# Six moves of x and the first queries' copy, put elsewhere in the order of a cross-attention kernel

## The chip, the cores and the metric

The kernel runs on one core of one Trainium2 chip. The metric is the device time of one execution in microseconds, as a median of several runs. Five engines work side by side, each through its own list in order: TensorE (PE, the matmuls), VectorE (DVE), ScalarE (ACT), GpSimd (POOL) and SyncE (SP). SP's list holds nearly all the DMA issues, so the order of the transfers is the order of SP's list. The work of each engine is written out by hand; nothing reorders it, and semaphores make an instruction wait until what it needs is there.

## What is computed

Layer norm of x, queries, attention over a memory of 256 slots whose keys and values are the same tensor, an output projection, and the residual. Batch 8, 256 queries, 256 slots, width 1024, 32 heads of 32, float32 throughout.

```python
mu = jnp.mean(hidden_states, axis=-1, keepdims=True)
var = jnp.var(hidden_states, axis=-1, keepdims=True)
x = (hidden_states - mu) * jax.lax.rsqrt(var + LN_EPS) * ln_gamma + ln_beta
Q = _split_heads(x @ Wq.T)
K = _split_heads(memory_keys)
V = _split_heads(memory_values)
scores = jnp.einsum('bhsd,bhtd->bhst', Q, K) * scale
mask = attention_mask[:, None, None, :]
scores = jnp.where(mask, scores, -jnp.inf)
probs = jax.nn.softmax(scores, axis=-1)
attn = jnp.einsum('bhst,bhtd->bhsd', probs, V)
...
out = attn @ Wout.T
return residual + out
```

## The kernel before

**Groups.** The work is cut into 64 groups: group n is batch n // 8 and four of its heads, that is 128 of the 1024 columns. For a group, PE makes the queries (L340), the scores of the four heads (L479, 128 queries by 256 slots, twice) and, two groups later, the values products (L622); DVE adds the mask and takes the minimum (L515), ACT takes the exponential and its sum (L519), DVE the reciprocal (L526), POOL multiplies by it (L528), and DVE transposes the probabilities in blocks of 32 (L534). The main loop's pass n holds, on PE, the scores of group n + 1, values of group n - 2, steps of the output projection (L694) and queries still to be made.

**Moves of probabilities.** The values products need half of the blocks in other partitions. ACT copies a part of them aside (`aside`, L540); then two DMAs move blocks within the tile pT (the first pair, L600) and two more bring in the copy (the second pair, L604). The second pair writes where the first has read, so it waits for the first to land. Between the two pairs SP issues what stands in the list `between`: the loads of later keys, values, x, output weights and residuals. All this is `tail`; for the first seven groups it is held back into the next group's softmax, from group 8 on it follows at once.

**x of a batch.** From the third batch on, x is normalized on ACT, transposed in blocks of 32 by DVE (`blocks_x`, L311, tile xe), and sixteen DMAs of 64 KB each (`move_x`, L327) bring the blocks to their partitions in tile xnT. The table `moves` says in which pass: for the third batch four in pass 5, six in pass 6, six in pass 7. They are issued behind the softmax of that pass. The first product that reads the third batch's xnT is the query of group 16, in pass 10.

**The start.** Before the loop, batch 0's x comes in halves of 128 queries. `transpose_x0` and `copy_x0` (L275 on ACT, L277 on DVE) bring it to tile xnT by eight chunks of 128 columns, `first_q` makes group 0's queries (L285) with a copy to qa by ACT (L289), and `scores(0, (0,))` the scores of the first half. The softmax of group 0 is a generator, so that the caller can put PE's and ACT's other work between its parts; `next(first)` runs it to its next `yield`. It carries a list `fill` of three pieces: statistics of batch 1's two halves (`ln_stats`: DVE L226, L229, L231, then a power on POOL, L234) and the normalization of its first half on DVE (`ln_norm`, L252). `fill_in()` takes the next piece. The second half is normalized by POOL (also L252) after the softmax of group 0, and PE transposes both halves (L302) at the end of pass 0.

SP's transfers share eight semaphores in turn.

Of the kernel before, what the change touches and what calls it, by code (L numbers as in the profile page):

```python
# [59 lines left out]
def xattn_kernel(  # L60
# [11 lines left out]
    nc = tc.nc  # L72
# [3 lines left out]
    NC = D // P  # L76
    NQ = NC
    NH = P // HD
# [191 lines left out]
    def copy_x0(s, c, engine):  # L270

        to, pt = xnT0[:, c, ts(s, P)], px0[s, c // (NC // 2)][:, c % (NC // 2), :]
        g, b = gam[:, c : c + 1], bet[:, c : c + 1]
        if engine is nc.scalar:
            nc.scalar.activation(to, pt, AF.Identity, bias=b, scale=g)  # L275
        else:
            nc.vector.tensor_scalar(to, pt, g, b, ALU.mult, ALU.add)  # L277

    def first_q(s, chunks=range(NC)):

        if s == 0:
            pqs[0] = ps_q.tile([P, 512], F32, tag="pq", name="pq_0")
        cols = ds(0, P) if s == 0 else ds(P, P + 1)
        for c in chunks:
            nc.tensor.matmul(  # L285
                pqs[0][:, cols], wq[:, 0, c, :], xnT0[:, c, cols],
                start=(c == chunks[0]), stop=(c == chunks[-1]),
            )
        nc.scalar.activation(qa[:, 0, cols], pqs[0][:, cols], AF.Copy, scale=NEG_SCALE)  # L289
# [194 lines left out]
    def softmax(*args):  # L484
        for _ in softmax_parts(*args):
            pass
# [4 lines left out]
    def softmax_parts(n, copies=(), ahead=(), between=(), hooks={}, fill=()):  # L491

        fill = list(fill)

        def fill_in():
            if fill:  # L500
                fill.pop(0)()

        pss = scs[n]
        pT = pTs[n] = ptp.tile([P, 2, NI, NH, NS, K], F32, tag="pT", name=f"pT_{n}")
        pc = asp.tile([P, NI, NH, NS, K], F32, tag="pc", name=f"pc_{n}")
        es, mns, dens = {}, {}, {}

        def exps(j, part=range(NS)):
            if 0 in part:
                es[j] = ep.tile([P, NS, T], F32, tag="e", name=f"e_{n}_{j}")  # L510
                mns[j] = sm.tile([P, NS], F32, tag="mn", name=f"mn_{n}_{j}")
                dens[j] = sm.tile([P, NS], F32, tag="den", name=f"den_{n}_{j}")
            e, mn, den = es[j], mns[j], dens[j]
            for s in part:
                nc.vector.tensor_tensor_reduce(  # L515
                    out=e[:, s, :], in0=pss[j][:, s, :], in1=mbs[n // NQ], scale=1.0,
                    scalar=NO_SCORE, op0=ALU.add, op1=ALU.min, accum_out=mn[:, s : s + 1],
                )
                nc.scalar.activation(  # L519
                    e[:, s, :], e[:, s, :], AF.Exp, bias=mn[:, s : s + 1], scale=-1.0,  # L520
                    accum_out=den[:, s : s + 1],
                )

        def normalize(j):
            rden = sm.tile([P, NS], F32, tag="rden", name=f"rden_{n}_{j}")
            nc.vector.reciprocal(rden, dens[j])  # L526
            for s in range(NS):
                nc.gpsimd.tensor_scalar(  # L528
                    es[j][:, s, :], es[j][:, s, :], rden[:, s : s + 1], 1.0,
                    ALU.mult, ALU.mult,  # L530
                )

        def blocks(j):
            nc.vector.transpose(  # L534
                pT[:, :, :, j, :, :].rearrange("p a i s k -> p (a i) s k"),
                es[j].rearrange("p s (b t) -> p b s t", t=K),
            )

        def aside(j):
            nc.scalar.copy(pc[:, :, ts(j, 2)], pT[:, 1, :, ts(j, 2)])  # L540

        if n == 0:
            for j in range(NH - 1):
                exps(j, (0,))
            yield
            exps(NH - 1, (0,))
            fill_in()
            yield
            for j in range(NH):
                exps(j, (1,))  # L550
            normalize(0)
            fill_in()
        else:
            exps(0)
            while tails:
                tails.pop()()
            late = "p1" in hooks
            if not late:
                for done in list(pvs):
                    copy_at(done)  # L560
            exps(1)
            for hook in hooks.get("soon", ()):
                hook()
            exps(2)
            normalize(0)
            for hook in hooks.get("p1", ()):
                hook()
            exps(3)
            if late:
                for done in list(pvs):  # L570
                    copy_at(done)
        copies = list(copies)
        for copy in copies[: NQ if n <= NQ else 1 if n == NQ + 1 else 0]:
            copies.remove(copy)
            copy()
        for hook in hooks.get(0, ()):
            hook()
        normalize(1)
        fill_in()
        blocks(0)  # L580
        for hook in hooks.get(1, ()):
            hook()
        normalize(2)
        fill_in()
        blocks(1)
        aside(0)
        normalize(3)
        fill_in()
        blocks(2)
        while fill:  # L590
            fill_in()
        for copy in copies:
            copy()

        def tail():
            blocks(3)
            aside(1)

            for r in range(2):
                nc.sync.dma_start(pT[ts(2 * r, K), 1], pT[ts(2 * r + 1, K), 0])  # L600
            for load in between:
                load()
            for r in range(2):
                nc.sync.dma_start(pT[ts(2 * r + 1, K), 0], pc[ts(2 * r, K)])  # L604

        for load in ahead:
            load()
        if n < NQ or N - NQ < n < N - 1:
            tails.append(tail)
        else:  # L610
            tail()
        yield
# [16 lines left out]
    def copy_at(n):  # L629
        b, c = divmod(n, NQ)  # L630
        k, c = divmod(c, NK)
        if c == 0:
            ats[b, k] = atp.tile([P, NK, NS, NA, K], F32, tag="at", name=f"at_{b}_{k}")
        for r, pv in enumerate(pvs.pop(n)):
            nc.scalar.copy(  # L635
                ats[b, k][:, c, :, ts(r, 2), :], pv.rearrange("p a s k -> p s a k")
            )
# [136 lines left out]
    for n in range(N):  # L774
# [12 lines left out]
    loads, stats, norms, trans, moves, biases, masks = (  # L787
        {n: [] for n in range(N)} for _ in range(7)
    )
    for b in range(1, B):  # L790
        first = NQ * (b - 1) + 2
        if b == 1:
            when = dict(moves=())
        elif b == 2:
            when = dict(
                loads=(0, 1), stats=(2, 3), norms=(3, 3), trans=(4, 5),
                moves=tuple(5 + (i + 2) // 6 for i in range(16)),
            )
        else:
# [4 lines left out]
                moves=tuple(first - 6 + (i + 2) // 6 for i in range(16)),  # L804
# [60 lines left out]
    transpose_x0(1)  # L865
    scores(0, (0,))
    for c in range(NC):
        copy_x0(1, c, nc.scalar if c < NC // 2 else nc.vector)
    first = softmax_parts(0, (partial(copy_q, 1), partial(copy_q, 2)), (), (), {}, [
        partial(ln_stats, 1, 0), partial(ln_stats, 1, 1),  # L870
        partial(ln_norm, 1, 0, nc.vector),
    ])
    next(first)
    first_q(1)
    make_q(1, second=True, chunks=range(2))
    next(first)
# [9 lines left out]
    for b in range(B - 1):  # L886
        done, ends = 0, b == B - 2
        for i, counts in enumerate(ENDS if ends else STEPS):
            n = NQ * (b + 1) + i
# [15 lines left out]
    for n in range(N):  # L905
        b, i = divmod(n - NQ, NQ)
        new_q = new_qs[n]
        between = []
# [5 lines left out]
        if n + 3 in firsts or n + 2 in firsts:  # L914
            between, ahead = between + ahead, []
# [11 lines left out]
            between.append(partial(load_wo, which, pair))  # L927
        if n == NQ - 1:
            between.append(partial(load_res, 0, 0, 0))
        if n == N - 4:  # L930
            again = xp.tile([P, NS, D], F32, tag="x", name="x_again")
            for s in range(NS):
                between.append(partial(nc.sync.dma_start, again[:, s, :], x[B - 1, ts(s, P), :]))
# [88 lines left out]
        if N - NQ + 2 < n < N - 1:  # L1022

            c = n - (N - NQ + 3)
# [104 lines left out]
```

## Time and profile before

| | us |
|---|---|
| median of 3 runs | 577.44 (575.85 to 577.75) |
| profiled execution, device time | 575.24 |
| its span | 573.5 |
| PE busy | 565.9 (99%) |
| DVE busy | 459.2 (80%) |
| ACT busy | 412.3 (72%) |
| POOL busy | 403.8 (70%) |
| DMA queue of SP, share of 16 engines' span | 68.9% |

A line of the time line gives the start and the duration in microseconds, the engine, the line of the kernel, the operation, the tiles written and read, the shape, and how many instructions were merged; in brackets stands how long the engine had been idle before and what ended that. SPq are issues of transfers: the transfer itself lands later. PE's matmuls overlap, so the sum of durations in a row can exceed the time to the next row. In the list of waits a line names who waited, for what, the total in microseconds, how often, and the longest.

### The profile page before, as it was taken

The numbers are of one execution on the slowest core, as the hardware profiler recorded it, in microseconds if no ns is written. First come the engines' busy times: TensorE is split into PE (matmuls) and PEld (weight loads), VectorE is DVE, ScalarE is ACT, GpSimd is POOL, SyncE is SP. The second block draws the span as 40 slices with busy tenths as digits, with TensorE's granted clock in tenths as the row PEclk, the third lists the DMA queues.
The fourth block names the chain that finished last, engine by engine and source line by source line (L and its number), as shares of the span: only waits on it lengthen the run. The fifth ranks groups of instructions, "written<-read, shape, count | busy, mean of one in ns | idle before, by whom it ended". The sixth has DMA issues, their size and how long they took to land.

```text
span 573.5 us, 20000 instructions
## 1 busy us (share of the span) xinstructions
PE 565.9 (99%) x7162; PEld 392.1 (68%) x7162; DVE 459.2 (80%) x1698; ACT 412.3 (72%) x1424; POOL 403.8 (70%) x675
## 2 busy tenths in 40 slices
PE   8999999899999999999999999999999999999997
PEld 8788876566667677677676677667766777755444
DVE  6897987788877879888888888888877868879823
ACT  4688886767758867698667967769767876869920
POOL 1788898789896896776567675666657667448780
PEclk9999999999999999999999999999999999999999
DMA  8675877766678667877787767886768774536751
GB/s 299 238 201 189 241 216 216 240 186 189 192 239 273 195 181 220 248 241 204 202 239 208 214 196 192 251 263 190 181 177 258 210 228 141 142 101 180 212 162 74
DMA packets 47475, 117.98 MB, mean 206 GB/s; under 512 B 9104, under 2 KB 9872, under 8 KB 47376
## 3 DMA queue, kind: packets, MB, share of 16 engines
q1 hardware_dynamic: 47088, 116.69, 68.9%
q8 instruction: 57, 0.93, 0.7%
q14 instruction: 42, 0.34, 0.2%
q10 hardware_dynamic: 288, 0.01, 0.0%
HBM read 65.28 MB, written 11.53 MB: 134 GB/s over the span
## 4 chain that ended last, share of the span: by engine, by line
PE 86%; POOL 4%; DVE 4%; DMA 2%; ACT 1%; issue 1%; SPq 1%; DVEq 0%; ACTq 0%; POOLq 0%
PE po_S L694 20%; PE pq_A L440 16%; PE pv L622 11%; PE sc L479 10%; PE po_A L694 10%; PE pq L340 7%; PE pq_S L440 6%; PE po_end L761 3%; POOL e L528 3%; DVE e L515 2%; DMA pT<-pT 1%; PE po_last L761 1%; ACT e L519 1%; PE busy L120 1%; DVE pT L534 1%
## 5 line engine op out<-in xcount | busy, mean ns | idle before, releaser
L528 POOL TENSOR_SCALAR e<-e,rden 128x256 f32<-128x256 f32 x512 | 235.8, 478 | 128.7 <-DVE rden L526 127.0
L519 ACT ACTIVATE e<-e,mn 128x256 f32<-128x256 f32 x512 | 254.1, 501 | 51.2 <-DVE mn L515 50.8
L534 DVE STREAM_TRANSPOSE pT<-e 128x512 f32<-128x512 f32 x256 | 180.7, 707 | 53.1 <-POOL e L528 35.5
L515 DVE CUSTOM_DVE_ANT_0 e<-sc,mb 128x256 f32<-128x256 f32 x512 | 185.9, 416 | 26.9 <-PE sc L479 26.4
L540 ACT COPY pc<-pT 128x512 f32<-128x512 f32 x128 | 79.0, 617 | 68.7 <-DVE pT L534 41.2
L519 ACT ACTIVATION_READ_ACCUMULATOR e<-e,mn 128x1 f32 x512 | 97.9, 191 | 0.0
L340 PE MATMUL pq<-xnT,wq 128*128 128x256 f32 (+1 forms) x368 | 84.2, 383 | 2.1 <-DMA xnT<-xe 2.1
L340 PEld LDWEIGHTS pq<-xnT,wq 128*128 128x128 f32 x368 | 68.6, 190 | 16.8 <-issue 6.9
L622 PE MATMUL pv<-pT,v 64*32 64x128 f32 x4096 | 74.8, 274 | 1.0 <-issue 0.8
L622 PEld LDWEIGHTS pv<-pT,v 64*32 64x32 f32 x4096 | 57.1, 105 | 26.7 <-issue 12.7
L479 PEld LDWEIGHTS sc<-k,qa 32*128 32x128 f32 x1024 | 46.2, 184 | 42.4 <-issue 23.2
L694 PE MATMUL po_S<-wo,at 128*128 128x512 f32 x152 | 74.3, 606 | 0.0
L479 PE MATMUL sc<-k,qa 32*128 32x256 f32 x1024 | 73.6, 400 | 0.1
L694 PE MATMUL po_A<-wo,at 128*128 128x512 f32 x128 | 60.9, 609 | 0.0
L694 PE MATMUL po_S<-wo,s 128*128 128x512 f32 x104 | 50.1, 606 | 0.0
L526 DVE RECIPROCAL rden<-den 128x2 f32<-128x2 f32 x256 | 37.6, 147 | 6.0 <-ACT e L519 4.8
L515 DVE DVE_READ_ACCUMULATOR2_ANT mn<- 128x1 f32 x512 | 42.4, 83 | 0.0
L440 PEld LDWEIGHTS pq_A<-xnT,wq 128*128 128x128 f32 x320 | 37.3, 192 | 4.8 <-issue 4.1
L694 PEld LDWEIGHTS po_A<-wo,at 128*128 128x128 f32 x128 | 22.5, 189 | 24.6 <-issue 22.7
L694 PEld LDWEIGHTS po_S<-wo,at 128*128 128x128 f32 x152 | 25.8, 190 | 19.8 <-issue 19.1
L440 PE MATMUL pq_A<-xnT,wq 128*128 128x128 f32 x320 | 37.3, 275 | 0.0
L635 ACT COPY at<-pv 128x128 f32<-128x128 f32 x128 | 26.2, 254 | 8.2 <-PE pv L622 8.2
(95 smaller groups left out, 605.1 us busy)
## 6 DMA issues: line engine op xcount, KB each, us to landing
v<-in_kv_dram SPq DMA_DIRECT2D x32, 512.0 KB, 4.4
pT<-pT SPq DMA_DIRECT2D x128, 128.0 KB, 2.9
pT<-pc SPq DMA_DIRECT2D x128, 128.0 KB, 4.1
ring<-kept_T SPq DMA_DIRECT2D x18, 512.0 KB, 5.3
k<-in_kv_dram SPq DMA_DIRECT2D x32, 256.0 KB, 3.7
x<-in_x_dram SPq DMA_DIRECT2D x14, 512.0 KB, 5.6
r<-in_x_dram SPq DMA_DIRECT2D x28, 256.0 KB, 5.1
out_dram<-r SPq DMA_DIRECT2D x28, 256.0 KB, 2.5
```

What stands on the lines that cost most here:

```text
L340: nc.tensor.matmul(pqs[n], wq[:, o, c, :], xnTs[b](c), start=(c == 0), stop=(c == NC - 1),)
L440: nc.tensor.matmul(pqs[b][:, o, :], w[:, c], x_[:, c], start=begins and o + c == 0, stop=c == NK - 1, skip_group_check=True,)
L479: nc.tensor.matmul(scs[n][j][:, s, :], qa[r, n % NQ, ts(s, P)], ks[n - n % 2][r, n % 2, :], start=True, stop=True,)
L515: nc.vector.tensor_tensor_reduce(out=e[:, s, :], in0=pss[j][:, s, :], in1=mbs[n // NQ], scale=1.0, scalar=NO_SCORE, op0=ALU.add, op1=ALU.m ...
L519: nc.scalar.activation(e[:, s, :], e[:, s, :], AF.Exp, bias=mn[:, s : s + 1], scale=-1.0, accum_out=den[:, s : s + 1],)
L526: nc.vector.reciprocal(rden, dens[j])
L528: nc.gpsimd.tensor_scalar(es[j][:, s, :], es[j][:, s, :], rden[:, s : s + 1], 1.0, ALU.mult, ALU.mult,)
L534: nc.vector.transpose(pT[:, :, :, j, :, :].rearrange("p a i s k -> p (a i) s k"), es[j].rearrange("p s (b t) -> p b s t", t=K),)
L540: nc.scalar.copy(pc[:, :, ts(j, 2)], pT[:, 1, :, ts(j, 2)])
L622: nc.tensor.matmul(pvs[n][r][j * HD : (j + 1) * HD], vs[n - n % 2][ts(r, 2 * K), i, ds(n % 2 * P + j * HD, HD)], pT[ts(r, 2 * K), :, i, j, ...
L635: nc.scalar.copy(ats[b, k][:, c, :, ts(r, 2), :], pv.rearrange("p a s k -> p s a k"))
L694: nc.tensor.matmul(po, operand(b, name)[:, c], wo[:, which, c], start=begins and c == 0, stop=c == NK - 1, skip_group_check=not begins,)
```

## The change

Three edits. In the softmax of group 0 the exponentials of all four heads of the first half are issued in one stretch, with one `yield` behind them, and the `fill_in()` that stood behind the fourth is gone. The caller's first `next(first)` goes too, so `first_q(1)`, with its copy on ACT, and two chunks of the next queries come ahead of all these exponentials. The three pieces of `fill` are then taken behind `normalize(0)`, `normalize(1)` and `normalize(2)`; before, they were taken behind the fourth exponential of the first half, `normalize(0)` and `normalize(1)`.

The eight copies of the second half of batch 0's x go to ACT and DVE in turn; before, ACT had the first four and DVE the last four.

In pass 7 (NQ is 8) the six moves of the third batch's x are put at the head of `between`, ahead of the load of values and of a residual, and so between the two pairs of moves of group 8's probabilities; the table's entry is emptied, so they are not issued again behind the softmax.

```diff
         if n == 0:
-            for j in range(NH - 1):
+            for j in range(NH):
                 exps(j, (0,))
-            yield
-            exps(NH - 1, (0,))
-            fill_in()
             yield
             for j in range(NH):
                 exps(j, (1,))
...
     for c in range(NC):
-        copy_x0(1, c, nc.scalar if c < NC // 2 else nc.vector)
+        copy_x0(1, c, nc.vector if c % 2 else nc.scalar)
     first = softmax_parts(0, (partial(copy_q, 1), partial(copy_q, 2)), (), (), {}, [
         partial(ln_stats, 1, 0), partial(ln_stats, 1, 1),
         partial(ln_norm, 1, 0, nc.vector),
     ])
-    next(first)
     first_q(1)
     make_q(1, second=True, chunks=range(2))
     next(first)
...
         if n == NQ - 1:
             between.append(partial(load_res, 0, 0, 0))
+            between[:0] = [partial(move_x, *args) for args in moves[n]]
+            moves[n] = []
```

## The prediction

> **What bounds the kernel now.** First the page's head, for how much room TensorE (PE) has; then the list of waits, for where the rest goes; then the time lines round each place that the change touches.
>
> ```profile
> span 573.5 us, 20000 instructions
> PE 565.9 (99%) x7162; PEld 392.1 (68%) x7162; DVE 459.2 (80%) x1698; ACT 412.3 (72%) x1424; POOL 403.8 (70%) x675
> ...
> PE pq L340 <- DMA xnT<-xe: 2.1, 1, 2.1
> ```
>
> PE is idle for 573.5 - 565.9 = 7.6 us in all. One wait of 2.1 us is for the moves of x (the columns are the total, how often, the longest). It is the third batch's first query product; PE's time line has it:
>
> ```profile
> 99.32 1.22 PE L622 MATMUL pv<-pT,v 64*32 64x128 f32 x64
> ...
> 103.70 3.69 PE L340 MATMUL pq<-xnT,wq 128*128 128x256 f32 x16 [2.11 <-DMA xnT<-xe]
> ```
>
> At 99.32 stand the values products of group 8, which need both pairs of moves of group 8's probabilities. Without the wait, the query product would start 103.70 - 2.11 - 99.32 = 2.27 us after them. SyncE's queue (SP) before this, and what it waited for:
>
> ```profile
> 85.55 0.43 SPq L173 DMA_DIRECT2D wo<-in_woT_dram  x1
> ...
> 87.33 1.19 SPq L600 DMA_DIRECT2D pT<-pT  x2
> 88.57 0.57 SPq L144 DMA_DIRECT2D v<-in_kv_dram  x1
> 89.19 0.49 SPq L150 DMA_DIRECT2D r<-in_x_dram  x1
> 94.61 1.95 SPq L604 DMA_DIRECT2D pT<-pc  x2
> 96.61 3.75 SPq L327 DMA_DIRECT2D xnT<-xe  x6
> ...
> SPq L604 <- DMA pT<-pT: 4.8, 1, 4.8
> ...
> SPq L327 <- DMA wo<-in_woT_dram: 2.2, 1, 2.2
> ```
>
> Group 8's first pair is issued at 87.33, then v and r; the second pair (94.61) stands 4.8 us until the first has landed; only then come the six moves, 0.63 us apart. The last line shows a move of x that waits 2.2 us for a weight load with which it shares no data: eight semaphores go round among SP's transfers, so an issue also waits until the one eight issues before it has landed.
>
> At the start GpSimd (POOL) is the pace:
>
> ```profile
> 15.96 0.55 POOL L234 TENSOR_TENSOR rstd<-ve,mhalf 128x1 f32<-128x1 f32 x1 [6.72 <-DVE ve L231]
> ...
> 19.02 1.11 POOL L234 TENSOR_TENSOR rstd<-ve,mhalf 128x1 f32<-128x1 f32 x1 [0.67 <-DVE rden L526]
> 20.12 2.74 POOL L528 TENSOR_SCALAR e<-e,rden 128x256 f32<-128x256 f32 x6
> 22.85 3.78 POOL L252 TENSOR_SCALAR x<-x,mv,rstd 128x1024 f32<-128x1024 f32 x1
> ...
> 26.63 1.03 PE L302 MATMUL px<-ring,x 128*128 128x128 f32 x8
> ```
>
> POOL normalizes the second half of batch 1's x until 26.63, and PE's transposes of it start right there; from there the chain of what ended last runs through POOL's next normalizations, DVE and ACT to PE's first values product at 36.66.
>
> **The start, part by part.** *Copies in turn.* Now ACT does four from 11.07 and DVE four from 11.50 (1.37 us), idle 0.92 us before them. In turn, DVE can begin with chunk 1 as soon as ACT has chunk 0, near 11.07, and is done at 12.45 instead of 12.87. PE does not notice: its product of these chunks starts at 12.04, behind the scores, in both orders. Worth 0 to PE; DVE's 0.4 us goes into a wait, below.
>
> *The query copy ahead of four exponentials.* PE ends that product near 14.09 (12.04 + 2.05). ACT now copies it at 14.73, behind three exponentials; then at 14.11, and the exponentials follow at 14.28, 14.77, 15.27, 15.76 (0.495 apart, as in its rows). The fifth then starts at 16.25, exactly as now (16.25), so nothing is lost there. PE's second half of the first scores, now 15.04, can start at 14.88: a gain of 0.15 us as long as nothing later holds PE.
>
> *What goes with the removed fill.* DVE's first layer-norm statistics of batch 1 (two of 0.69, then 0.21 and 0.15: 1.7 us with the hand-overs) fill 14.16 to 15.87 now, while DVE would otherwise wait for those scores. After, DVE stands from 13.8 to 15.64, and every statistic moves down one place. Step by step, DVE: minima 15.64 to 17.09, reciprocal to 17.17, statistics of half 0 to 18.79, reciprocal to 18.86, statistics of half 1 to 20.49, blocks (0.71) to 21.12, reciprocal to 21.17, normalization of half 0 (0.80) to 21.88, blocks to 22.5, reciprocal to 22.55. POOL: rstd 18.88 to 19.43, probabilities of head 1 to 20.34, rstd 20.58 to 21.13, head 2 from 21.26, head 3, then x. Head 2 meets DVE's normalization on 21.09 to 21.88, as the rstd at 19.02 does now, which took 1.11 in place of 0.55; I add that 0.56 to head 2, which then ends at 22.8, head 3 at 23.72, and x (3.78) at 27.48 in place of 26.63. **+0.85 us**: PE, there at 26.48, waits a microsecond, and the chain to 36.66 moves with it. [...] Bounds: at best the start gains 0.15 plus the 0.46 by which the values at 36.18 (1.62) exceed the 1.16 of most rows of values: -0.6; at worst all 1.7 us of moved statistics show.
>
> **The six moves.** They pass v, r and the second pair on SP; nothing on POOL's queue moves. After 87.33 the first three go out at 88.57, 89.2, 89.8. The fourth waits for the weight load eight issues before it (issued 85.55; such loads take up to 7.7 us to land in this stretch): 93.2. The fifth and sixth wait for the second pair of group 7 in the same way, 93.8 and 94.4; the last lands some 2.0 us later (what each of the six takes now), near 96.4 in place of 103.46. The 2.11 us wait is gone. But v, now 88.57, goes out near 95.1, behind the first pair's landing, r at 95.7, and the second pair at 96.3 and 96.9 in place of 94.61 and 95.22. Behind the second pair stand group 9's moves (100.47 now, about 97.6 then) and a load of k: earlier, no harm. r is first read at 102.0 by DVE and should land by then.
>
> What is late next is the pair. Unknown is its landing. With an idle queue ahead of it, as now, it takes 2.8 to 3.1 us, which gives 100.0. Where v and r go out just before a pair, as they then will, the trace has 3.9 (issues at 108.17) and 4.2 to 4.5 (at 121.26): 100.8 to 101.4. I take 3.9, the row with the same order: 100.8, so the values start 1.5 us after their present 99.32, and this part is worth -2.11 + 1.5 = **-0.6 us**; ends -1.4 (landing 100.0) and, for the longest row of such a move, the 7.3 us that the chain shows for the first pair, 104.2 - 99.32 - 2.11 = +2.8. [...]
>
> **Sum.** +0.85 - 0.6 = +0.25 us. Both parts move SP and PE alike, so they add. After 103.70 PE has no wait until the end, so the sum passes to the end one to one. The profiled execution took 575.24 us (span 573.5 and 1.74 round it), 2.2 under the median of the runs, 577.44; on the median I get 577.7.
>
> **Rivals.** *The pair lands late (slower).* Wait for x exchanged for a longer wait for probabilities at the values of group 8. For: SP's second pair then has 384 KB of moves, 512 KB of v and 256 KB of r just ahead, and the first pair in a full queue took 7.3 us. Against: by 95 the queue has run dry (DMA share 0.37 from 95 to 97). Price at the long end: +2.8 + 0.85 = +3.65, 581.1. It decides from a landing of 5.5 us (102.4) on, where the whole is +1.8.
>
> *The start costs nothing and the pair lands in 3.1 (faster).* For: ACT's exponentials end at the same time in both orders. Against: POOL's chain above. -1.4 + 0 = 576.0, and with the small waits at the start gone, 575.4.
>
> *The moves come no earlier.* If the weight load held SP to the end, the start's +0.85 alone is left: 578.3. Against: three moves need no such landing.
>
> **How the numbers follow.** About 0.3% (1.7 us) is what a measurement of this kernel can tell from no change; the three runs shown spread over 1.9 us. The forecast has 0.42 (0.35 within, 0.05 slower, 0.02 faster), the late pair 0.33 (all slower), the free start 0.22 (0.20 faster, 0.02 within), moves no earlier 0.03 (within). Faster 0.22, same 0.40, slower 0.38. The range, 575.4 to 580.4, reaches from the free start's lower value into the late pair's price and leaves out some 0.08 below and 0.12 above.
>
> **What would show it.** PE's wait L340 on xnT gone, a wait before the values of group 8 near 100 in its place (on pT<-pc); the fourth move some 3 us after the third; v near 95; POOL's L252 ending near 27.5 and PE idle about 1 us in the transposes L302; DVE idle 1.8 us from 13.8. I am wrong if POOL ends x by 26.6 (then the start is free), or if the pair lands under 3 us or over 5.5 after its issue.

## The result and the profile after

The changed kernel takes 579.67 us in the median (577.33 to 583.69, 20 executions) against 576.57 us (574.81 to 580.02, 20 executions) for the kernel before beside it. The ratio is 1.0053, with a 95% interval of 1.0036 to 1.0070: slower by 0.53%, some 3.05 us. Repeated beside another experiment it was 1.0060 (1.0038 to 1.0083). The forecast was 577.7 us, about even. The measured time lies inside its range, which reached to 580.4.

The changed kernel's lines behind L540 have moved up by three: the pairs of moves are L597 and L601, the values L619, the projection L691.

The page's head and PE's list of waits, of the changed kernel:

```profile
span 575.7 us, 19995 instructions
PE 567.1 (99%) x7162; PEld 392.6 (68%) x7162; DVE 459.7 (80%) x1698; ACT 412.5 (72%) x1424; POOL 403.8 (70%) x675
...
PE pv L619 <- DMA pT<-pc: 2.8, 1, 2.8
...
PE px L302 <- POOL x L252: 0.6, 1, 0.6
```

The wait for x is gone, as forecast. In its place stands a longer one, 2.8 us, for the second pair of moves of group 8's probabilities, and a new one of 0.6 us at the start. This execution took 577.45 us, among the fastest of the changed kernel. PE's busy sum is 1.2 us higher than before too, since rows whose inputs trickle in are stretched and count as busy throughout: the start's second product L285 takes 2.70 us in place of 2.05, the values of group 8 1.65 in place of 1.22. SP's time line round the six moves:

```profile
88.44 1.16 SPq L597 DMA_DIRECT2D pT<-pT  x2
89.66 6.36 SPq L327 DMA_DIRECT2D xnT<-xe  x6
96.06 1.92 SPq L144 DMA_DIRECT2D v<-in_kv_dram  x1
98.03 0.43 SPq L150 DMA_DIRECT2D r<-in_x_dram  x1
98.50 1.14 SPq L601 DMA_DIRECT2D pT<-pc  x2
```

The six moves occupy SP for 6.36 us; three go out at once (89.66, 90.29, 90.94), and the fourth, at 94.24, has waited 2.7 us for the weight load eight issues before it. So v, r and the second pair go out late. The last transfer of the pair, issued at 99.06, landed at 103.55, 4.5 us later; the values begin shortly before, at 103.16, and are stretched:

```profile
99.18 1.15 PE L479 MATMUL sc<-k,qa 32*128 32x256 f32 x16
103.16 1.65 PE L619 MATMUL pv<-pT,v 64*32 64x128 f32 x64 [2.84 <-DMA pT<-pc]
```

The third batch's first query product starts at 105.70 in place of 103.70, 2.0 us late.

The other place is the start. ACT's and DVE's time lines of the eight copies that now take turns, and POOL's normalization behind them:

```profile
11.06 0.46 ACT L275 ACTIVATE xnT<-px,bet,gam 128x128 f32<-128x128 f32 x1 [0.16 <-PE px L266]
11.99 0.81 ACT L275 ACTIVATE xnT<-px,bet,gam 128x128 f32<-128x128 f32 x2 [0.48 <-DVE xnT L277]
13.28 0.46 ACT L275 ACTIVATE xnT<-px,bet,gam 128x128 f32<-128x128 f32 x1 [0.48 <-DVE xnT L277]
```

```profile
11.55 0.41 DVE L277 TENSOR_SCALAR xnT<-px,gam,bet 128x128 f32<-128x128 f32 x1 [0.95 <-ACT xnT L275]
12.49 0.76 DVE L277 TENSOR_SCALAR xnT<-px,gam,bet 128x128 f32<-128x128 f32 x2 [0.53 <-ACT xnT L275]
13.78 0.41 DVE L277 TENSOR_SCALAR xnT<-px,gam,bet 128x128 f32<-128x128 f32 x1 [0.53 <-ACT xnT L275]
```

```profile
24.18 3.77 POOL L252 TENSOR_SCALAR x<-x,mv,rstd 128x1024 f32<-128x1024 f32 x1
```

In the kernel before, the same eight copies ran side by side:

```profile
11.07 1.50 ACT L275 ACTIVATE xnT<-px,bet,gam 128x128 f32<-128x128 f32 x4 [0.16 <-PE px L266]
11.50 1.37 DVE L277 TENSOR_SCALAR xnT<-px,gam,bet 128x128 f32<-128x128 f32 x4 [0.92 <-PE px L266]
```

Now each engine stands idle about 0.5 us, twice each, while the other makes one copy (0.41 or 0.46 us), and the last copy ends at 14.19, not at 12.87. The chunks lie in two tiles of PSUM (where this kernel has PE's products), 0 to 3 in the first and 4 to 7 in the second. ACT's two copies from 11.99 are chunks 2 and 4; only chunk 4, the first of the second tile, runs beside a copy of DVE's (chunk 3, from 12.49). POOL's L252 ends at 27.95 instead of 26.63.

The profiled executions differ by up to 1.1 us in when PE's second product L285 starts (11.80 to 12.90). Counted from that start, L252 ends 14.59 us later in the kernel before (26.63 - 12.04) and 15.92 us later in the changed one (27.95 - 12.03). That number repeats to 0.02 us from profile to profile, and the experiments on the start are read by it.

### The profile page after: what moved, and what is told of

It is laid out like the page before. It is cut to its first block, busy times and chain, and to the rows that moved or that the text cites. A ratio compares the mean times of both kernels' runs of the same rounds, so it can differ in the third digit from the quotient of the medians.

```text
span 575.7 us, 19995 instructions
## 1 busy us (share of the span) xinstructions
PE 567.1 (99%) x7162; PEld 392.6 (68%) x7162; DVE 459.7 (80%) x1698; ACT 412.5 (72%) x1424; POOL 403.8 (70%) x675
## 4 chain that ended last, share of the span: by engine, by line
PE 84%; DMA 8%; POOL 2%; ACT 2%; DVE 1%; SPq 1%; issue 1%; DVEq 0%; ACTq 0%
PE po_S L691 20%; PE pq_A L440 16%; PE pv L619 11%; PE sc L479 10%; PE po_A L691 10%; PE pq L340 7%; PE pq_S L440 6%; PE po_end L758 3%; DMA wq<-in_wq_dram 2%; DMA x<-in_x_dram 2%; DMA wo<-in_woT_dram 1%; DMA xnT<-xe 1%; PE po_last L758 1%; ACT e L519 1%; POOL e L528 1%
## 5 line engine op out<-in xcount | busy, mean ns | idle before, releaser
L540 ACT COPY pc<-pT 128x512 f32<-128x512 f32 x128 | 79.0, 617 | 69.3 <-DVE pT L534 42.2
L619 PE MATMUL pv<-pT,v 64*32 64x128 f32 x4096 | 75.2, 274 | 3.6 <-DMA pT<-pc 2.8
L619 PEld LDWEIGHTS pv<-pT,v 64*32 64x32 f32 x4096 | 57.3, 105 | 29.6 <-issue 12.4
L691 PE MATMUL po_S<-wo,at 128*128 128x512 f32 x152 | 74.3, 606 | 0.0
L691 PE MATMUL po_A<-wo,at 128*128 128x512 f32 x128 | 60.9, 609 | 0.0
L691 PE MATMUL po_S<-wo,s 128*128 128x512 f32 x104 | 50.1, 605 | 0.0
L691 PEld LDWEIGHTS po_A<-wo,at 128*128 128x128 f32 x128 | 22.5, 189 | 24.6 <-issue 22.7
L691 PEld LDWEIGHTS po_S<-wo,at 128*128 128x128 f32 x152 | 25.8, 190 | 19.8 <-issue 19.1
```

Of the source, the lines that this page charges most:

```text
L619: nc.tensor.matmul(pvs[n][r][j * HD : (j + 1) * HD], vs[n - n % 2][ts(r, 2 * K), i, ds(n % 2 * P + j * HD, HD)], pT[ts(r, 2 * K), :, i, j, ...
L691: nc.tensor.matmul(po, operand(b, name)[:, c], wo[:, which, c], start=begins and c == 0, stop=c == NK - 1, skip_group_check=not begins,)
```

## The experiments

Every edit is made on the kernel before, unless another base is named.

**The six moves alone.**

```diff
             between.append(partial(load_res, 0, 0, 0))
+            between[:0] = [partial(move_x, *args) for args in moves[n]]
+            moves[n] = []
```

> Before, with the six moves alone put at the head of the list between the two pairs. Theory (each part has its own price): PE's first values product stays at 36.2, x is no longer waited for, and the values of group 8 wait 2.3 to 3.0 us for their second pair in its place, so that the third batch's first query starts 0.3 to 0.9 us after the 103.70 of before; time +0.5 to +2 us. Rival (the loss of the whole change is the start's): the wait for the pair is under 1.5 us, the query starts before 103.2, time -0.5 us or less. Fourth move some 3 us after the third in both.

578.08 us against 576.93: ratio 1.0027 (1.0014 to 1.0041). SP did what the forecast had worked out, within 0.6 us: the fourth move at 92.68, v at 94.50, r at 95.87, the pair at 96.35 and 96.91. But PE waited 2.37 us ahead of the values of group 8, which then started at 101.22, and 0.20 within them: 2.57 for the pair, where 1.5 was forecast, against 2.11 for x before. (The list of waits names an exponential on ACT there, which ended at about the same moment; what these values wait for are the two transfers of the pair, and the second landed at 101.66.) That is 0.46 us more waiting, and the kernel lost 1.5 by the ratio. The table by stretches of this kernel (the fields are the stretch, its length, the busy time of each engine, then the granted clock, the DMA share and GB/s) has the rest:

```profile
98.85:101.22 2.37, 0.00 (x1) 0.03 (x2) 2.30 (x11) 0.99 (x4) 1.18 (x3) 1.00 1.09 258
101.22:101.74 0.52, 0.37 (x2) 0.10 (x2) 0.32 (x2) 0.48 (x2) 0.52 (x1) 1.00 0.89 169
101.74:105.15 3.41, 3.36 (x64) 2.37 (x65) 0.00 (x0) 1.34 (x6) 1.52 (x2) 0.50 0.58 131
105.15:110.00 4.85, 4.85 (x20) 3.61 (x19) 3.83 (x16) 2.44 (x10) 2.89 (x7) 1.00 0.89 278
```

PE idles from 98.85 to 101.22, and from 101.74 to 105.15 its clock is granted at half. By the granted 0.50, PE does the work of 1.7 in these 3.41 us. The rows agree: the projection L694 at 103.68, two matmuls, takes 1.84 us, four fifths of it at half clock, against 1.12 in the kernel before (100.47, granted 1.00). The waits do not show this loss; it is a part of PE's "busy" time.

**The exponentials behind the query copy alone.**

```diff
-            for j in range(NH - 1):
+            for j in range(NH):
                 exps(j, (0,))
             yield
-            exps(NH - 1, (0,))
-            fill_in()
-            yield
...
-    next(first)
     first_q(1)
```

> Before, with the exponentials behind the queries' copy alone, copies of x as before, moves as before. Theory: POOL ends batch 1's x (L252) near 27.5 in place of 26.63, the first values product starts near 37.0 in place of 36.2; about 0.4 of this is made good at the values of group 6 (idle 0.85 us before), so +0.4 to +0.9 us at the end. Rival (the copies in turn are the start's only price): L252 ends by 26.8 and the time is that of before.

576.58 us against 576.93: ratio 0.9997 (0.9981 to 1.0013), no difference that shows. L252, though, ends 15.28 us after the product's start (27.58 - 12.30), so 0.69 later than before, and PE waits 0.62 us in the transposes L302. The local loss is there, and near the forecast's 0.85. Why it does not show in the median is taken up below.

**The copies in turn alone.**

```diff
-        copy_x0(1, c, nc.scalar if c < NC // 2 else nc.vector)
+        copy_x0(1, c, nc.vector if c % 2 else nc.scalar)
```

> Before, with the copies in turn alone. Theory (a copy on one engine waits until the other engine's copy out of the same PSUM tile has ended): the eight copies end near 14.2 in place of 12.87, PE's query product of the second half lasts 2.7 in place of 2.05 us, DVE's chain behind it moves by about 1.3 us, L252 ends near 27.9 and the first values product starts near 37.4; +0.8 to +1.3 us at the end. Rival (the copies' delay falls into waits that stand there anyway): the copies end near 14.2, but L252 ends by 26.9.

578.02 us against 576.93: ratio 1.0022 (1.0008 to 1.0035). L252 ends 15.93 us after the product's start (28.62 - 12.69): 1.33 later than before, just what the whole change does there. PE's second half of the first scores, in this kernel's time line, waits for the copied queries, which stand behind three exponentials that themselves started late:

```profile
17.03 0.71 PE L479 MATMUL sc<-k,qa 32*128 32x256 f32 x8 [0.76 <-ACT qa L289]
```

**Two copies at a time, but each engine out of a tile of its own.** The same eight copies by the same two engines, issued alternately; ACT has chunks 0 to 3, in the first PSUM tile, DVE 4 to 7, in the second.

```diff
-    for c in range(NC):
+    for c in (0, 4, 1, 5, 2, 6, 3, 7):
         copy_x0(1, c, nc.scalar if c < NC // 2 else nc.vector)
```

> Before, with the eight copies issued alternately for ACT and DVE as in the change, but each engine keeps to its own PSUM tile (ACT chunks 0 to 3, DVE 4 to 7). Theory (the price of the copies in turn is that two engines take turns at one PSUM tile): the copies end 0.8 to 0.9 us after PE's query product of the second half begins, as before, the product lasts 2.05 us, and the time is that of before within its interval. Rival (alternating the issue itself costs): the product lasts 2.7 us, +1 us or more.

576.49 us against 576.14: ratio 0.9996 (0.9975 to 1.0016). DVE's copies run in one piece (11.96 to 13.33) and L252 ends 14.59 us after the product's start (27.08 - 12.49), as before. Each engine's own list is then the same as before; only the order in which the two lists were written differs. So alternating the issue costs nothing here, nor does the use of two engines. What is left is that both read one tile: in the copies in turn every wait is for the other engine's copy out of the same tile, put there by the program's semaphores, and the one copy out of the other tile did not wait.

**The six moves between the pairs, but behind v and r.** First on the kernel before:

```diff
             between.append(partial(load_res, 0, 0, 0))
+            between += [partial(move_x, *args) for args in moves[n]]
+            moves[n] = []
```

> Before, with the six moves between the two pairs, but behind v and r in place of ahead of them. Theory (what makes the pair late is that v and r go out six moves later, behind the landings that the moves stand for): v and r stay at 88.6 and 89.2, the moves go out from 89.8 to 95.6, the second pair near 96 and lands near 99.5, the values of group 8 wait under 0.6 us and the query waits for nothing: -1.5 to -2.1 us. Rival (any six transfers ahead of the pair make it as late): the values wait 2 us or more, time as e1.

575.50 us against 576.93: ratio 0.9979 (0.9965 to 0.9994), faster. In its profile neither the values of group 8 nor the query waits, as expected; the gain, 1.2 us by the ratio, is a little under the 1.5 expected. The same order in the changed kernel, start included:

```diff
-            between[:0] = [partial(move_x, *args) for args in moves[n]]
+            between += [partial(move_x, *args) for args in moves[n]]
```

> The whole change, with the six moves behind v and r in place of ahead of them. Theory (the parts add): the start's price stays, the moves' loss turns into the gain seen when they alone stood behind, so 0.0 to 0.2% above before, 2 to 3 us under the changed kernel. Rival (with the start late the moves' place does not matter): 0.4% or more above before.

577.78 us against 576.14: ratio 1.0021 (1.0003 to 1.0038). The wait at the values of group 8 is 1.06 us, and L252 ends 15.92 us after the product's start. The order gains here too, from 1.0053 to 1.0021, but not as much as the 0.9979 of the moves and the 1.0022 of the copies would give together. These 0.21% stand at the upper end of the theory's 0.0 to 0.2%, and the interval stays just under the rival's 0.4%.

**Which half of the late pair counts: its late issue, or its slow landing?** Three moves ahead of v and r, the other three behind the second pair, so that the fourth move holds nothing up:

```diff
             between.append(partial(load_res, 0, 0, 0))
+            (bx, part), = moves[n]
+            between.insert(0, partial(move_x, bx, part[:3]))
+            moves[n] = [(bx, part[3:])]
```

> Before, with the first three moves ahead of v and r and the other three behind the second pair, where they are now. Two causes of the late pair: its issue waits behind moves 4 to 6, which wait for earlier landings (1.7 us in the run of the moves alone), and v and r stand right ahead of it in the queue (another 1.7 us to land). If the issue is what counts: pair out near 95, landed near 99 to 99.5, no wait over 0.5 us, time -1 to -2 us. If v and r ahead count as much: the pair, out at the same time, still lands near 100 or later, values wait 0.7 us or more, time within 0.7 us of before.

574.90 us against 576.14: ratio 0.9978 (0.9952 to 1.0003). The pair goes out at 95.57 and 96.12, close to where it was before, yet v and r stand right ahead of it, and its last transfer lands at 102.34, 6.2 us later. PE's time line still has a wait there, put down to "issue", and a stretched row behind it; the pair is all that these values wait for:

```profile
101.97 1.59 PE L622 MATMUL pv<-pT,v 64*32 64x128 f32 x64 [1.70 <-issue]
```

So the trace has the second theory's wait, but the median is the first theory's: 1.2 us faster than before (the interval just includes no change). The next version is the fairer comparison for the landing. There the pair goes out at the same time, counted from the start of L285 (83.3 us after it here, 83.4 there), behind the same v, r and three moves, but with v and r issued some 5.6 us earlier, and it lands after 4.0 us. So late loads ahead of the pair are enough for a late landing here, 6.2 us against 4.0. How much of the loss they make, the two medians do not settle.

**The version that takes away both.** v and r first, as before, then three moves, the pair, three moves:

```diff
             between.append(partial(load_res, 0, 0, 0))
+            (bx, part), = moves[n]
+            between.append(partial(move_x, bx, part[:3]))
+            moves[n] = [(bx, part[3:])]
```

> Before, with three moves behind v and r and three behind the second pair. Both causes taken away: v and r stay at 88.6 and 89.2, the pair goes out near 95 and lands within 3.2 us, the last move lands near 100; neither the values nor the query wait: -1.5 to -2.2 us, at least as fast as all six behind v and r. If it is slower than that one, the place of the last three moves counts and not the pair.

573.99 us against 576.14: ratio 0.9956 (0.9933 to 0.9979). SP's and PE's time lines:

```profile
89.42 0.44 SPq L150 DMA_DIRECT2D r<-in_x_dram  x1
89.91 4.86 SPq L327 DMA_DIRECT2D xnT<-xe  x3
95.41 1.14 SPq L604 DMA_DIRECT2D pT<-pc  x2
96.59 2.79 SPq L327 DMA_DIRECT2D xnT<-xe  x3
```

```profile
101.89 1.16 PE L622 MATMUL pv<-pT,v 64*32 64x128 f32 x64
102.97 1.13 PE L694 MATMUL po_A<-wo,at 128*128 128x512 f32 x2
103.94 3.40 PE L340 MATMUL pq<-xnT,wq 128*128 128x256 f32 x15
```

The pair lands at 99.94, the last move at 100.84; neither the values nor the query product waits. This is the best version found, by its median, and the idea of the change (the moves ahead of the pair) is right when v and r keep their place.

**The best version again, and with the exponentials' order added.**

> The three-behind order again (v, r, three moves, the second pair, three moves), the same kernel: the ratio to the kernel before was 0.9956, with an interval of 0.9933 to 0.9979 from three rounds. Theory that the late pair and the wait for x are both taken away: 0.994 to 0.998 again, 1.2 to 3.5 us. Rival, that the first run was the luck of few executions: within 0.2% of before.

```diff
+            (bx, part), = moves[n]
+            between.append(partial(move_x, bx, part[:3]))
+            moves[n] = [(bx, part[3:])]
...
-            for j in range(NH - 1):
+            for j in range(NH):
                 exps(j, (0,))
             yield
-            exps(NH - 1, (0,))
-            fill_in()
-            yield
...
-    next(first)
```

> The kernel before with v, r, three moves, the second pair, three moves on SP in pass 7, and with the four exponentials behind the query copy at the start, the removed fill with them. Theory that the start's loss is there and was only taken up by the two waits on transfers further on (2.11 us for x, the second pair of group 8): with these waits gone, the +0.69 us by which POOL's L252 ended later in the run of the exponentials alone reaches the end, so this is slower than the three-behind kernel of the same call by 0.4 to 0.9 us. Rival, that it is lost earlier, in the values of group 6 that wait for their pair anyway: equal to it within 0.3 us. Below the kernel before by 1.5 to 2.2 us by the theory, by 2.2 to 3 by the rival.

The best version repeated: 575.26 us against 576.11, ratio 0.9970 (0.9949 to 0.9992), a smaller gain than the first time, but a gain; in this profile the pair takes 4.8 us to land, at 100.9, though v and r went out 7 us before it, and the values of group 8 wait 0.92 us. So the late pair is not always taken away. With the exponentials' order added: 576.04 us, ratio 1.0000 (0.9976 to 1.0025). The difference of the two, 0.8 us, has the size of the 0.70 us by which L252 again ends late (15.29 against 14.59 after the product's start). Their intervals overlap, so this points to the start's loss reaching the end rather than shows it, and the gain of 1.5 to 2.2 us over the kernel before, which the theory expected of this version, did not come.

**Is the half clock a cost of its own?** In the changed kernel, matmuls that serve nothing are put ahead of the values of group 6 and of group 8, into the PSUM tile that the values then overwrite:

```diff
         pT = pTs.pop(n)
+        for i in range({6: 12, 8: 16}.get(n, 0)):
+            m = n + 3
+            nc.tensor.matmul(
+                pvs[n][i % 2].rearrange("p a s k -> p (a s k)"),
+                qa[:, m % NQ, ts(0, P)], ks[m - m % 2][:, m % 2, :P],
+                start=True, stop=True,
+            )
```

> The changed kernel with idle work for PE just ahead of two values products: 12 extra matmuls (128*128 128x128, about 0.13 us each, 1.6 us) ahead of those of group 6 and 16 (2.1 us) ahead of those of group 8, written into the tile that the values then overwrite. They stand where PE waits for the pairs of moves, so they take time only where the wait is shorter than they are. Theory that a part of the loss is TensorE's clock, which runs at half for 3.41 us (1.7 us of work) behind a wait of PE of about 2 us: of the executions of the changed kernel 17 of 20 had a mean granted clock of 0.997 or less; here at most a third have, and the median is 0.5 to 2 us below that of the changed kernel run beside it. Rival, that these stretches at half clock come of themselves and the longer times with them: as many executions at 0.997 and below as in the kernel beside it, and the median equal to it or above it by up to 1 us.

> The changed kernel itself again, to stand beside the one with the extra matmuls: 1.0053 of the kernel before with an interval of 1.0036 to 1.0070 the first time. By both theories 2 to 4 us above the kernel before; by the theory of the clock with more executions at 0.997 and below than the kernel before has (18 of 35, 13 of 31 and 10 of 23 in the earlier comparisons).

With the extra matmuls 579.61 us, ratio 1.0069 (1.0043 to 1.0096); the changed kernel beside it 579.61 us, ratio 1.0060. Six executions of six had the full clock (0.999 or 1.0 in the mean); of the changed kernel beside it one of nine. On the clock, then, the expectation held. On the time it did not, and the reason is in PE's time line of the kernel with the extra matmuls:

```profile
102.24 3.84 PE L618 MATMUL pv<-k,qa 128*128 128x128 f32 x32
106.00 1.16 PE L626 MATMUL pv<-pT,v 64*32 64x128 f32 x64
```

Each matmul of these shapes is two instructions (x32 for 16), which I had counted as one. The two fillings took 2.9 and 3.8 us in place of 1.6 and 2.1, more than the waits that they were to cover, and what the clock gave back seems to have gone into them: at full clock this kernel is 2.1 us slower than the changed kernel's four executions at full clock (577.5). So the run shows that the stretches go when PE is kept busy, not what they cost. A filling of the right length was not tried.

## Where the time went

The stretches at half clock are all of one length, 3.41 us, so an execution's mean granted clock counts them: 3.41 / 2 / 575 is 0.003, so I read 0.997 as one of them and 0.994 as two. The profiled executions of the moves alone and of the changed kernel's second time have 0.997 and one stretch each. (A shorter one in the last microseconds costs 0.001 at most; in the kernel before 0.60 us of it lie in the span.) In the profiles they stand in two places only, behind the values of group 6 (starting at 84.62 to 87.53, after waits of 1.41 to 2.45 us) and behind those of group 8 (starting at 101.74 and 104.73, after 2.37 and 1.66). None stands where PE had not waited, but not every wait is followed by one: the 2.11 us of the kernel before and the 2.84 of the changed kernel's profile were not.

The traces' record of the granted clock tells most of the difference. In every trace the clock first rises to full between 5.1 and 7.3 us, and from there the full stretch ahead of a half one is a whole number of 3.413 us: 23, 24, 28 or 29 of them. It is so too ahead of the short one at the end: in the profile of the kernel before the clock is full from 6.24 us on for 566.61 us, 166 times 3.4133, and in the changed kernel from 6.22 for 570.03, 167 times. So in these traces the clock changes on a grid, and where a wait falls in it matters. Cut the 14 traces into these windows and add up PE's idle time in each: the six windows with 1.83, 1.84, 2.04, 2.28, 2.35 and 2.52 us were each followed by a half stretch, and of the others, all but one had 1.71 us or less. The 2.84 us of the changed kernel's profile fell into two windows, with 1.47 and 1.51. The one exception is the wait for x in the kernel before, 1.89 us in one window without a half stretch; why, the traces do not say. On this reading an execution can gain or lose a stretch by where its grid lies.

| kernel | executions, with at least one stretch | stretches per execution |
|---|---|---|
| before, the comparisons that list it | 103, of which 47 | 0.49 |
| changed (both times) | 29, of which 25 | 1.17 |
| changed, PE kept busy | 6, none | 0 |
| changed, moves behind v and r | 12, of which 8 | 0.67 |
| six moves alone | 12, of which 10 | 1.17 |
| exponentials' order alone | 12, of which 2 | 0.17 |
| copies in turn alone | 12, of which 8 | 0.67 |
| copies by tile | 10, of which 6 | 0.60 |
| six moves behind v and r | 12, of which 5 | 0.50 |
| three moves ahead | 12, of which 3 | 0.25 |
| best version (both times) | 20, of which 4 | 0.20 |
| best version, exponentials' order too | 12, of which 4 | 0.42 |

About what a stretch costs can be read off the kernel before: its 44 executions with one took 577.25 us in the median, the 56 without 575.86, so 1.4 us more, a part of which may be the wait ahead of the stretch.

By this count the changed kernel has 0.68 stretches more than the kernel before, 0.68 x 1.7 = 1.2 us. The rest is lost at full clock: executions without a stretch took 577.5 us in the median (four of them) against 575.3 to 576.1 for the kernel before, 1.4 to 2.2 us. The traces, both without a stretch of that length, have 2.0 us at the third batch's first query: 1.33 of the start, less 0.4 that the values of group 6 would have waited anyway (they waited 0.85 us in two pieces before, 0.47 after), plus 2.84 - 2.11 = 0.73 of longer waiting for the pair and 0.43 by which the values' row is stretched (2.1 by these terms). With the clock's 1.2 that is 3.2 us, for 3.05 measured. The terms at full clock are those of one execution: in the second profile of the changed kernel the values of group 6 waited 2.17 us and those of group 8 only 1.82. So the agreement is in part luck. Firmer is that the two edits that lose alone, the moves (1.5) and the copies (1.25), add up to 2.8.

The same count comes near for the parts. The six moves alone have 0.57 stretches more than the 0.60 of the kernel before beside them: 1.0 us and 0.46 us of waiting, 1.4 against 1.5 measured. But their two executions at full clock took 577.44 us, already 1.35 above the 576.09 of the kernel before at full clock, so how the loss divides between waiting and clock is not shown. The copies have nearly as many as before, and their 1.33 us reach the end as they are (1.25 measured). The exponentials' order alone has 0.43 fewer, worth 0.7 us, which is what it lost at the start: in the median it came out even. At full clock it took 576.44 us, 0.35 more than the 576.09 of the kernel before, so some of the loss is there. The fewer stretches there may be luck, or may come from the shorter wait for x (1.71 us in its profile); twelve executions do not tell.

## Why the prediction was right or wrong

The measured time lies in the stated range, but only because the range was drawn out towards the late pair's price; the sum was wrong in three places: the copies at the start, the late pair, and the clock, for which it had no term.

*Copies in turn, "worth 0 to PE": wrong, the largest local error at the start.* The step let DVE begin with chunk 1 as soon as ACT had chunk 0, and end at 12.45; it ended at 14.19. Copies out of one PSUM tile run one behind the other here, each engine idle about 0.5 us while the other copies. The trace after shows the same in code that was not changed, among the first half's copies, where ACT's last waits 0.19 us for DVE (9.58, after DVE's L277); the forecast asked when the data is there, not who else has the tile. Price 1.33 us at L252, 0.22% alone.

*The query copy ahead of the exponentials, +0.85: near, for that edit alone* (0.69; the scores' gain of 0.15 is there too, 2.85 us after the product's start in place of 3.00). The 0.56 us for head 2 beside DVE's normalization came as 0.48: of POOL's four multiplications in this row of that run, which take 0.47 us each elsewhere, one took 0.95. The changed kernel's trace shows where: the one from 21.87, which meets DVE's normalization (21.70 to 22.49), took 0.95, the three behind it 0.47 each.

```profile
21.50 2.32 POOL L528 TENSOR_SCALAR e<-e,rden 128x256 f32<-128x256 f32 x4
```

The wait in the transposes was 0.62 rather than a microsecond, and DVE's idle time 1.38 rather than 1.8. In the whole change this loss does not add to that of the copies: with late copies, L252 ends 15.92 or 15.93 after the product's start in either order. So the start's +0.85 was near the 1.33 for the wrong reason.

*The issue of the moves, v, r and the pair: right for the moves alone, too early for the whole.* For the moves alone all ten times are within 0.6 us, in part because two things cancelled: group 8's first pair went out 0.37 us earlier than before, and v's issue took 1.33 us in place of 0.57. In the whole change the pair went out at 98.50 and 99.06 in place of 96.3 and 96.9: the first pair was 1.1 us later, with the late start, which the sum took in by letting SP and PE move alike; the rest is v's issue, which took 1.92 us.

*The pair's landing, 3.9 us after its issue: too low.* It took 4.5 us in the changed kernel and about 4.8 with the moves alone. The rows of 4.2 to 4.5 were named and set aside for "the row with the same order". That was a misreading: in the row of 3.9 the load of the mask stands between r and the pair, and in the row of 121.26 (4.2 to 4.5) v and r stand right ahead of it, as in the change.

```profile
107.64 0.43 SPq L190 DMA_DIRECT2D mk<-in_mask_dram  x1
108.17 1.15 SPq L604 DMA_DIRECT2D pT<-pc  x2
```

The waiting was 2.57 us with the moves alone and 2.84 in the whole, so this part is not worth -0.6 at full clock but +0.46 and, with the stretched row, +1.2. Such moves land faster elsewhere: 2.2 us after the issue for the two issued at 116.19 in the kernel before, 2.30 for the one issued there at 105.89, and 2.29 for group 9's first pair in the repeated best version (issued at 99.95 and landed at 102.24, after v and r were in). Right behind v and r it was 4.5.

*"After 103.70 PE has no wait until the end, so the sum passes to the end one to one": right as it stands.* From that query product to the end of the span it is 469.8 us before (573.5 - 103.70) and 470.0 in the changed kernel (575.7 - 105.70). What the sum lacks is a term ahead of it: the half clock behind the waits of groups 6 and 8, by the count above 1.2 us. (In the traces that have one, it ends before that product or, in one, 0.9 us into it.) Gaps of 1.4 to 2.5 us were followed by such a stretch of 3.41 us, and what counted, but for one case (1.89 us), was whether 1.8 us or more of idle time fell into one window of the grid of 3.413 us.

*The rivals.* The late pair is the one that came nearest in kind and in time, though not by its condition: it was to decide from a landing 5.5 us after the issue, and 4.5 was enough, since the issue itself came 2.2 us later than reckoned (1.1 of them with the start) and the clock followed. The free start and moves that come no earlier both fell. Neither of the two signs of being wrong came (POOL ended x at 27.95, the pair landed after 4.5 us), so they were too coarse to catch an error of this size. *The sum* was too low by 2.8 us. By the steps it is 0.5 at the start (1.33 for 0.85), 1.8 for the pair (2.84 + 0.43 for 1.5) and 1.2 for the clock, less the 0.4 taken up at group 6: 3.1.

## What to carry to other kernels

Two engines that copied out of one PSUM tile in turn were slower here than each with a tile of its own (1.33 us at L252), so look for waits of one copy on the other before calling such a split free. A small transfer that PE will need should not go out right behind large loads: here the pair took 4.5 to 6.2 us to land so, against 2.8 to 3.1 in the kernel before, and it was best to put the loads first, then a part of what nobody waits for yet, then the small one (4.0 and 4.8 us, ratios of 0.9956 and 0.9970). And where PE waits some 2 us, reckon with a half-clock stretch behind it when the wait falls into one window of the clock (six of the seven windows here with 1.8 us or more of idle time had one), and compare the mean granted clocks of the executions before a difference under 1% is put down to the edit.

## What was not expected of the hardware

- The 3.41 us stretches at half clock behind waits of 1.4 to 2.5 us, in 47 of 103 executions of the kernel before, and that they lie on a grid of 3.413 us: a wait of 2.84 us that the grid cut in two had none. Keeping PE busy through the two waits removed them in six of six.
- A 128 KB move of a pair takes 2.2 to 3.1 us from issue to landing with little ahead of it, but 4.5 us in the changed kernel and 6.2 us with three moves ahead, both times with v and r right in front, and 4.0 and 4.8 us in the best version, with v and r 6 to 7 us ahead and three moves between.
- An issue can itself be slow: v's took 1.92 us on SP in the changed kernel and 1.33 us with the moves alone, where 0.57 is usual. What held it, the traces do not say.
